# Later normalization of the next batch's rows, and other places for a few loads, in a two-layer graph kernel

## The chip, the core and the metric

The kernel runs on one core of one Trainium2 chip. The metric is device time in microseconds (us) of one execution, lower is better. The median of 3 runs of the kernel before is 2356.52 us (2349.64 to 2357.53). The profile is of one further execution with a span of 2362.4 us.

## The reference, cut to what matters

32 graphs (batches) of 512 nodes and 512 features go through two layers; all is float32.

```python
# x, adj: (32, 512, 512); W: (512, 1024); Wqk: (512, 1024); Wv: (512, 512)
h = maximum(layernorm(x), 0)                       # layer 0
agg = (adj @ h) / maximum(sum(adj, -1), 1e-6)
x = x + relu(concat([h, agg], 2) @ W.T)
h = maximum(layernorm(x), 0)                       # layer 1
q, k = split(h @ Wqk); v = h @ Wv
agg = adj @ (k * mask)
w = mask * sum(q * agg, -1) / sqrt(512)
x = x + softmax(w, axis=1)[:, :, None] * v
```

## The kernel before

For every batch i TensorE goes through four stages of products, each done by seven instead of eight block products (Strassen's scheme, so every stage also needs sums of blocks before it, on VectorE and GpSimd):

- U(i): adj times the masked h of layer 1, 56 matmuls
- Y(i+1): h of layer 0 times half of W, 56 matmuls, for the next batch
- O(i): layer 0's output, 112 matmuls, in 14 steps of 8
- TV(i-1): layer 1's two products of h (a matrix made of Wq and Wk, and Wv), 98 matmuls, in 14 steps of 7

After O(i) come TV(i-1), U(i), Y(i+1) and O(i+1). The program orders the work of all engines by hand: `p.at(n, f)` puts f into the instruction streams just after step n of the stage.

In a stage of the kind of O the products share three PSUM tiles. `copy` is an instruction of ScalarE (ACT in the profile); a product that comes back to a tile has to wait for the copy of what stands in it.

```python
def product(name, terms, place, finish):
    # m(k, p, first): 2 terms of 4 or 8 matmuls into p, one step (yield) after each
    pp = mm_tile(...)
    yield from m(1, pp, True)            # O: steps 0, 1
    c11 = place(0, 0); copy(c11, pp)
    pr = mm_tile(...)
    yield from m(2, pr, True)            # steps 2, 3
    finish(0, 0, c11, pr, c11)
    yield from m(6, pp, False)           # steps 4, 5
    c12 = place(0, 1); copy(c12, pp)
    pq = mm_tile(...)
    yield from m(5, pq, True)            # steps 6, 7
    m5 = block(...); copy(m5, pq)
    yield from m(7, pp, False)           # steps 8, 9
    c22 = place(1, 1); copy(c22, pp)     # stands in ACT's stream between steps 9 and 10
    finish(1, 1, c22, m5, c22)
    yield from m(3, pq, False)           # steps 10, 11
    finish(0, 1, c12, pq, c12)
    yield from m(4, pp, False)           # steps 12, 13: waits for the copy of c22
    finish(1, 0, None, pp, None)
```

While TensorE works on batch i, the rows of batch i+2 are made ready. x and adj come in through two half tiles ("n", two buffers for both): x is normalized in place and written to DRAM, from where it is read back transposed; then adj comes into the same two buffers.

```python
def half_tile(name):
    return big.tile([P, 2, 512], F32, tag="n", bufs=2, name=name)

class FrontH:                     # h of layer 0
    def load(self, h): self.n[h] = half_tile(...); half_rows(self.n[h], x[self.b], h)    # 4 DMAs
    def stats(self, c): ...                                     # VectorE: bn_stats, bn_aggr
    def write(self, c):
        normalize(v, v, self.t, c)                              # ACT: Relu, scale rstd, bias nmr
        nc.sync.dma_start(out=self.to.d[c], in_=v)
# variance(t): rstd, VectorE then GpSimd (pow); shift(t): nmr, VectorE
class FrontA:                     # adj
    def load(self, h): self.n[h] = half_tile(...); half_rows(self.n[h], adj[self.b], h)  # 4 DMAs
    def sum(self, c): nc.scalar.activation(v, v, AF.Copy, accum_out=DEG[...])            # ACT
    def degrees(self, h): ...                                                            # VectorE
    def write(self, c): nc.scalar.activation(v, v, AF.Copy, scale=self.rdeg[...]); nc.sync.dma_start(...)
class FrontH1:                    # h of layer 1
    def keep(self): nc.sync.dma_start(out=self.x1, in_=X[self.b]...)   # x after layer 0, 1 MB to DRAM
    def write(self, c): normalize(...); nc.sync.dma_start(...)
    def mask(self, c): nc.scalar.activation(..., scale=mraw[...])
```

In layer 1's product TV, product 1 takes four PSUM tiles (of eight), product 2 four more, and product 5 takes over those of product 2 (steps 6 and 7). ACT copies product 1, product 6 and product 5 out of PSUM; product 3 (steps 10 and 11) waits for the copies of product 5 (`m_tv` in the profile).

The main loop, cut:

```python
weights, mvR = start()          # ends with the "joint product" of Wq and Wk; it also takes h1 of batch 0
for i in range(B):              # B = 32
    if i > 0:
        p = Plan()
        for n in range(4): p.at(2 * n + 1, stream.load)      # DMA of a weight block
        ...
        p.at(9, post.store, 0); p.at(11, post.store, 1)      # output of batch i-2, 4 DMAs each
        for k in range(4): p.at(2 + k, f1.inner_sums, k, 0, 7)   # VectorE, 1 to 2 us each
        if 1 < i and i + 2 < B:                              # i = 2 to 29
            fh = FH[i + 2]
            for c in range(C):                               # C = 4
                p.at(3 + c, fh.stats, c)
                p.at(8 + c, fh.write, c)
            p.at(6, variance, fh.t)
            p.at(7, shift, fh.t)
        p.at(11, th.turn, 0)
        if 1 < i and i + 2 < B:
            fa = FA[i + 2] = FrontA(i + 2)
            p.at(12, fa.load, 0)
            p.at(13, fa.load, 1)
        p.at(12, f.stats, 0); ...
        run(layer0_out(i, stream.take), 14, p)               # O(i)

        p = Plan()
        for c in range(C):
            p.at([2, 3, 5, 6][c], f.write, c)
            p.at(8 + c, f.mask, c)
        p.at(1, f.keep)
        if 1 < i and i + 2 < B:
            for h in range(2):
                for c in range(2): p.at(4 + 2 * h + c, fa.sum, 2 * h + c)
                p.at(7 + 2 * h, fa.degrees, h)
        ...
        run(layer1_tv(i - 1), 14, p)                         # TV(i-1)
    ...
    run(layer1_u(i), 7, p)                                   # U(i)
    run(layer0_y(i + 1), 7, p)                               # Y(i+1)
```

Of the kernel before, what the change touches and what calls it, by code (L numbers as in the profile page):

```python
# [22 lines left out]
def kernel(  # L23
# [37 lines left out]
    C = N // P  # L61
# [53 lines left out]
    def of(t):  # L115
        return lambda i: t[:, i]
# [526 lines left out]
    FH, FA, F1 = {}, {}, {}  # L643
# [6 lines left out]
    def chain(p, f, n):  # L650


        p.at(n(0), f.keep)
        p.at(n(0), f.stats, 2)
        p.at(n(0), shift, f.t, 0, 2)
        p.at(n(0), f.write, 0)
        p.at(n(1), f.stats, 3)
        p.at(n(1), variance, f.t, 2, 4)
        p.at(n(1), f.write, 1)
        p.at(n(2), shift, f.t, 2, 4)  # L660
        p.at(n(3), f.write, 2)
        p.at(n(3), f.mask, 0)
        p.at(n(4), f.write, 3)
        p.at(n(4), f.mask, 1)
        p.at(n(5), f.masked_sums, 0)
        p.at(n(5), f.mask, 2)
        p.at(n(6), f.mask, 3)

    def start():
# [3 lines left out]
        fa = FA[0] = FrontA(0)  # L673
# [9 lines left out]
        fh = FH[1] = FrontH(1)  # L683
# [45 lines left out]
        p = Plan()  # L729
# [23 lines left out]
        p = Plan()  # L753
# [39 lines left out]
        f = F1[0] = FrontH1(0)  # L793
# [7 lines left out]
        p = Plan()  # L801
# [34 lines left out]
        p.at(12, f.to.read, 0)  # L836
        p.at(13, f.to.read, 1)
        FH[2] = FrontH(2)
        p.at(4, FH[2].load, 0)
        p.at(6, FH[2].load, 1)  # L840
        run(None, 14, p)
        return [right_sums(outer)[k] for k in range(4)] + [right_sums(inner)[k] for k in range(4)], mv

# [5 lines left out]
    with tc.manual_schedule(engines=engines):  # L849
        weights, mvR = start()  # L850
        post = None
        for i in range(B):
# [3 lines left out]
            f = F1[i]  # L856
            if i > 0:

                p = Plan()
                for n in range(4):  # L860
                    p.at(2 * n + 1, stream.load)
                right_y = right_sums(of(Y[i]), nc.gpsimd)
                p.at(0, right_y[0])
                p.at(0, right_y[2])
                for k in (1, 3):
                    p.at(1 + k // 2, FA[i].sums, k, nc.gpsimd)
                    p.at(1 + k // 2, right_y[k])
                if i == 1:
                    for k, g in enumerate(weights[4:]):
                        p.at(3 + 2 * k, g)  # L870
                    fa = FA[2]
                    for h in range(2):
                        for c in range(2):
                            p.at(2 * h + c, fa.sum, 2 * h + c)
                            p.at(4 + 2 * h + c, fa.write, 2 * h + c)
                        p.at(2 + 2 * h, fa.degrees, h)
                    FH[3] = FrontH(3)
                    p.at(9, FH[3].load, 0)
                    p.at(10, FH[3].load, 1)
                f1 = F1[i - 1]  # L880
                for k in range(4):
                    p.at(k // 2, f1.sums, k)
                if post is not None:
                    for c in range(C):
                        p.at(2 + c, post.apply, c)
                    p.at(3, post.add_x1, 0)
                    p.at(5, post.add_x1, 1)
                    p.at(9, post.store, 0)
                    p.at(11, post.store, 1)
                for k in range(4):  # L890
                    p.at(2 + k, f1.inner_sums, k, 0, 7)
                if 1 < i and i + 2 < B:
                    fh = FH[i + 2]
                    for c in range(C):
                        p.at(3 + c, fh.stats, c)
                        p.at(8 + c, fh.write, c)
                    p.at(6, variance, fh.t)
                    p.at(7, shift, fh.t)
                if more:
                    th = FH[i + 1]  # L900
                    p.at(2, th.to.read, 1)
                    p.at(11, th.turn, 0)
                if 1 < i and i + 2 < B:
                    fa = FA[i + 2] = FrontA(i + 2)
                    p.at(12, fa.load, 0)
                    p.at(13, fa.load, 1)
                p.at(12, f.stats, 0)
                p.at(12, f.stats, 1)
                p.at(13, variance, f.t, 0, 2)
                run(layer0_out(i, stream.take), 14, p)  # L910


                post = Post(i - 1, F1[i - 1])
                p = Plan()
                p.at(0, f.stats, 2)
                p.at(0, shift, f.t, 0, 2)
                p.at(0, f.stats, 3)
                p.at(1, variance, f.t, 2, 4)
                if last:
                    p.at(1, FA[i].factor)  # L920
                p.at(3, shift, f.t, 2, 4)
# [4 lines that stand above are left out]
                for k in range(4):  # L926
                    p.at([10, 12, 12, 12][k], f.masked_sums, k)
                if 1 < i and i + 2 < B:
                    for h in range(2):
                        for c in range(2):  # L930
                            p.at(4 + 2 * h + c, fa.sum, 2 * h + c)
                        p.at(7 + 2 * h, fa.degrees, h)
                if i == 1:
                    fa = FA[3] = FrontA(3)
                    p.at(11, fa.load, 0)
                    p.at(13, fa.load, 1)
                    fh = FH[3]
                    for c in range(C):
                        p.at(4 + c, fh.stats, c)
                        p.at(9 + c, fh.write, c)  # L940
                    p.at(7, variance, fh.t)
                    p[9].insert(0, lambda t=fh.t: shift(t))
                if more:
                    p.at(3, th.turn, 1)
                    for k in range(4):
                        p.at(5 + k // 2, th.sums, k)
                p.at(8, f.to.read, 0)
                p.at(9, f.to.read, 1)
                for k in range(7):
                    p.at(12 + k // 4, post.recombine, k, 0, 0)  # L950
                run(layer1_tv(i - 1), 14, p)


            p = Plan()
# [7 lines left out]
            if i == 0:  # L962
                fh = FH[2]
                for c in range(C):
                    p.at(c, fh.stats, c)
                p.at(3, variance, fh.t)
                p.at(4, shift, fh.t)
                p.at(4, weights[0])
                p.at(5, fh.write, 0)
                p.at(6, fh.write, 1)  # L970
                p.at(5, weights[1])
            elif more:
                for k in range(7):
                    p.at(1 + k // 4, post.recombine, k, 1, 0)
                for c in range(C):
                    p.at(3 + c // 2, post.dot, c)
                p.at(5, post.scores)
                p.at(5, post.maximum)
                if i == 1:
                    for c in range(C):  # L980
                        p.at(3 + c, fa.sum, c)
                    p.at(5, fa.degrees, 0)
                elif i + 2 < B:
                    for c in range(C):
                        p.at(c, fa.write, c)
                if 1 < i and i + 3 < B:
                    FH[i + 3] = FrontH(i + 3)
                    p.at(6, FH[i + 3].load, 0)
            else:
                p.at(0, f.turn, 0)  # L990
                for k in range(3):
                    p.at(1, f.inner_sums, k, 0, 2)
                p.at(1, f.turn, 1)
                for k in range(4):
                    p.at(2 + k // 2, f.sums, k)
                p.at(4, f.inner_sums, 3, 0, 2)
                for k in range(4):
                    p.at(5 + k // 2, f.inner_sums, k, 2, 7)
# [3 lines left out]
            if more:  # L1002
                p = Plan()
# [14 lines left out]
                        p.at(3 + k // 2, post.recombine, k, None, 1)  # L1018
                p.at(2, FA[i].factor)
                if i == 0:  # L1020
                    p.at(0, fh.write, 2)
                    p.at(1, fh.write, 3)
                    p.at(4, weights[2])
                    p.at(6, weights[3])
                    FA[2] = FrontA(2)
                    p.at(2, FA[2].load, 0)
                    p.at(3, FA[2].load, 1)
                elif i == 1:
                    p.at(0, fa.degrees, 1)
                    for c in range(C):  # L1030
                        p.at(2 + c, fa.write, c)
                    FH[4] = FrontH(4)
                    p.at(5, FH[4].load, 0)
                    p.at(6, FH[4].load, 1)
                elif i + 3 < B:
                    p.at(0, FH[i + 3].load, 1)
# [3 lines left out]
        p = Plan()  # L1040
# [71 lines left out]
```

## Time and profile before

| | busy, us | share of the span |
|---|---|---|
| TensorE, matmuls (PE) | 2269.6 | 96% |
| TensorE, weight loads (PEld) | 1977.3 | 84% |
| VectorE (DVE) | 1988.7 | 84% |
| ScalarE (ACT) | 1026.2 | 43% |
| GpSimd (POOL) | 504.8 | 21% |

The DMA engines moved 463.65 MB, at a mean of 196 GB/s. Names in the profile are those of the tiles, without numbers: `pp_o` is the tile pp of stage O, `n` a half tile with x, `a` one with adj, `nmr` the bias of a normalization, `ptv` the PSUM tiles of TV. An arrow points from what is read to what is written. A line number such as L100 is often that of a helper: L100 is `copy`, L258 `normalize`, L467 the matmuls of TV, L130 those of the other stages.

### The profile page before, as it was taken

Reading aid. Unit: us, or ns where it says so; the run is one execution under the profiler, and the core shown is the slowest. Engines: PE = TensorE matmul, PEld = TensorE weight load, DVE = VectorE, ACT = ScalarE, POOL = GpSimd, SP = SyncE. Lnnn points to the kernel's source line nnn. Section 1 sums busy time; section 2 is a strip of 40 time slices with the busy share of each in tenths; the row PEclk is TensorE's granted clock in tenths of the full one; section 3 lists DMA queues with packets and bytes.
Section 4 is the critical chain, followed back from the end, with each engine's and each line's share of the span. In section 5 each row is a group of like instructions: output and inputs, shape, how many; then the busy total and the mean of one; then the engine's idle time right before and its main releaser. Section 6 shows DMA issues by size and latency. Waiting matters only on the chain.

```text
span 2362.4 us, 32559 instructions
## 1 busy us (share of the span) xinstructions
PE 2269.6 (96%) x10372; PEld 1977.3 (84%) x10372; DVE 1988.7 (84%) x3619; ACT 1026.2 (43%) x1903; POOL 504.8 (21%) x453
## 2 busy tenths in 40 slices
PE   7998999999999999999999999999999999999996
PEld 6787888888888888888888888888888888888885
DVE  6788888888888888888788888888888888888878
ACT  4454434444334444344444344443444443444332
POOL 0212222112222122222022221222220222211222
PEclk9999999999999999999999999999999999999998
DMA  9877777887777887777877777777778777787552
GB/s 225 236 196 209 200 185 186 218 217 198 197 185 198 222 217 187 204 186 203 220 198 199 185 198 209 210 201 201 177 208 220 210 200 190 184 218 201 147 135 71
DMA packets 409594, 463.65 MB, mean 196 GB/s; under 512 B 37680, under 2 KB 271152, under 8 KB 405328
## 3 DMA queue, kind: packets, MB, share of 16 engines
q1 hardware_dynamic: 400176, 428.56, 68.0%
q0 software_dynamic: 8928, 32.51, 7.5%
q8 instruction: 82, 1.34, 0.3%
q14 instruction: 88, 0.72, 0.1%
q10 hardware_dynamic: 320, 0.52, 0.1%
HBM read 293.93 MB, written 167.51 MB: 195 GB/s over the span
## 4 chain that ended last, share of the span: by engine, by line
PE 43%; DVE 33%; DMA 11%; issue 5%; SPq 4%; ACT 2%; POOL 1%; DVEq 0%; ACTq 0%
PE ptv L467 26%; DVE h1T L97 11%; PE pp_o L130 6%; DVE tv L94 6%; PE pp_u L130 5%; DMA daT<-a 4%; DVE st L242 3%; DMA n<-in_x_dram 3%; DVE aT L280 3%; SPq L212 2%; PE pr_u L130 2%; DVE h1T L94 2%; DVE y L94 1%; SPq L204 1%; POOL rstd L248 1%
## 5 line engine op out<-in xcount | busy, mean ns | idle before, releaser
L467 PE MATMUL ptv<-mv,h1T 128*128 128x256 f32 x3136 | 682.6, 379 | 1.4 <-DVE h1T L97 1.2
L467 PEld LDWEIGHTS ptv<-mv,h1T 128*128 128x128 f32 x3136 | 595.7, 190 | 83.1 <-DVE h1T L97 1.6
L94 DVE TENSOR_TENSOR tv<-tv 128x256 f32<-128x256 f32 (+1 forms) x644 | 321.8, 511 | 11.6
L100 ACT ACTIVATE tv<-ptv 128x512 f32<-128x512 f32 (+1 forms) x372 | 189.5, 540 | 259.2 <-PE ptv L467 254.8
L130 PE MATMUL pp_o<-w,wide 128*128 128x256 f32 x992 | 246.8, 393 | 53.8 <-ACT o L100 53.8
L97 DVE TENSOR_TENSOR h1T<-h1T 128x512 f32<-128x512 f32 (+2 forms) x195 | 292.0, 1511 | 1.2
L130 PEld LDWEIGHTS pp_o<-w,wide 128*128 128x128 f32 x992 | 191.3, 195 | 91.0 <-ACT o L100 65.0
L130 PE MATMUL pp_o<-y,aT 128*128 128x256 f32 x1024 | 248.4, 386 | 1.1 <-POOL y L97 1.1
L130 PE MATMUL pp_y<-wide 128*128 128x256 f32 x1024 | 242.8, 380 | 0.0
L130 PE MATMUL pp_u<-h1m,aT 128*128 128x256 f32 x1024 | 242.0, 379 | 0.0
L130 PEld LDWEIGHTS pp_o<-y,aT 128*128 128x128 f32 x1024 | 200.2, 196 | 30.6 <-POOL y L97 1.5
L97 POOL TENSOR_TENSOR y<-y 128x512 f32<-128x512 f32 x124 | 217.8, 1757 | 19.2 <-DVE y L94 15.8
L130 PEld LDWEIGHTS pp_y<-wide 128*128 128x128 f32 x1024 | 195.0, 191 | 26.8 <-ACT y L100 0.3
L130 PEld LDWEIGHTS pp_u<-h1m,aT 128*128 128x128 f32 x1024 | 194.5, 190 | 27.1 <-issue 0.5
L248 POOL TENSOR_TENSOR rstd<-rstd,mhalf 128x2 f32<-128x2 f32 (+1 forms) x96 | 78.6, 819 | 545.1 <-DVE rstd L247 545.1
L548 POOL PARTITION_ALL_REDUCE gtop<-top x32 | 12.5, 392 | 854.0 <-DVE top L545 836.1
L100 ACT ACTIVATE y<-pp_y 128x512 f32<-128x512 f32 x128 | 76.4, 597 | 238.4 <-PE pp_y L130 238.4
L258 ACT ACTIVATE n<-n,nmr,rstd 128x512 f32<-128x512 f32 x120 | 91.0, 804 | 176.7 <-DVE nmr L252 173.8
L100 ACT ACTIVATE xu<-pp_u 128x512 f32<-128x512 f32 x128 | 76.4, 597 | 194.5 <-PE pp_u L130 194.5
L94 DVE TENSOR_TENSOR tv<-ptv,tv 128x512 f32<-128x512 f32 x248 | 142.6, 612 | 17.1 <-PE ptv L467 13.4
L100 ACT ACTIVATE o<-pp_o 128x512 f32<-128x512 f32 x96 | 56.7, 591 | 216.9 <-PE pp_o L130 216.9
L94 DVE TENSOR_TENSOR tv<-ptv,m_tv 128x512 f32<-128x512 f32 (+1 forms) x124 | 76.7, 623 | 80.8 <-PE ptv L467 68.3
(113 smaller groups left out, 3457.7 us busy)
## 6 DMA issues: line engine op xcount, KB each, us to landing
w<-dw SPq DMA_DIRECT2D x217, 256.0 KB, 3.2
xu<-in_x_dram SPq DMA_DIRECT2D x128, 256.0 KB, 5.0
a<-in_adj_dram SPq DMA_DIRECT2D x256, 128.0 KB, 3.5
dx<-xu SPq DMA_DIRECT2D x32, 1024.0 KB, 5.2
dh1T<-h1m SPq DMA_DIRECT2D x128, 256.0 KB, 4.3
sh1T<-dh1T SPq DMA_DIRECT2D x256, 128.0 KB, 3.2
shT<-dhT SPq DMA_DIRECT2D x248, 128.0 KB, 4.4
daT<-a SPq DMA_DIRECT2D x124, 256.0 KB, 3.0
```

The costliest lines, as they stand in the source:

```text
L94: (on or nc.vector).tensor_tensor(o, a, b, op=ALU.add)
L97: (on or nc.vector).tensor_tensor(o, a, b, op=ALU.subtract)
L100: nc.scalar.activation(o, i, AF.Copy)
L130: nc.tensor.matmul(p[:, rc, :], lt[:, LEFT[k], dk, ts(rc, P)], right[:, dk, :], start=first and n == 0, stop=True, skip_group_check=True,)
L204: nc.sync.dma_start(out=t[q * R:(q + 1) * R, :, :], in_=rows[:, 2 * h:2 * h + 2, :])
L212: nc.sync.dma_start(out=t[q * R:(q + 1) * R, :, :], in_=src[:, :, ts(q, P)].rearrange("k r j -> r k j"))
L242: nc.vector.bn_stats(st, src)
L248: nc.gpsimd.tensor_tensor(rstd[:, a:b], rstd[:, a:b], mhalf[:, a:b], op=ALU.pow)
L258: nc.scalar.activation(o, i, AF.Relu, scale=t[1][:, c:c + 1], bias=t[2][:, c:c + 1])
L280: nc.vector.transpose(o, self.s.pop(h).rearrange("p k (c r) -> p k c r", r=R))
L467: nc.tensor.matmul(banks[n][:, :, ts(i, P)], left[:, LEFT[k], LEFT_IN[j], :], mvR[:, RIGHT[k], RIGHT[j], :, :], start=first and i == 0, st ...
L548: nc.gpsimd.partition_all_reduce(self.gtop, self.top, channels=P, reduce_op=ReduceOp.max)
```

## The change

The change has five parts. It adds and removes no instruction; all move.

- In O(i), i from 2 to 29, the normalization and the write of the next rows of x move two steps later, from steps 8 to 11 to steps 10 to 13, and with them the small operations before them (variance from 6 to 7, shift from 7 to 9). Its aim is that the normalization stands at the end of O in place of its middle.
- For the same i the second half of adj is asked for in step 1 of TV, behind the 1 MB write of `keep`, in place of step 13 of O.
- In the joint product at the start, `keep` of batch 0 stands two places later (behind the first two writes of h1), and the loads of batch 2's x stand at 10 and 12 in place of 4 and 6.
- Batch 2's rows of x are measured two steps later in U(0), and all four are normalized and written in Y(1) in place of two in U(0) and two in Y(1); one load of adj and the sums of weights there move with them.
- In O(1) the sums, degrees and writes of batch 2's adj stand two steps later, the loads of batch 3's x one step later.

```diff
@@ chain: joint product
-        p.at(n(0), f.keep)
+        p.at(n(2), f.keep)
@@ start: joint product
-        p.at(4, FH[2].load, 0)
-        p.at(6, FH[2].load, 1)
+        p.at(10, FH[2].load, 0)
+        p.at(12, FH[2].load, 1)
@@ O(1)
-                            p.at(2 * h + c, fa.sum, 2 * h + c)
-                            p.at(4 + 2 * h + c, fa.write, 2 * h + c)
-                        p.at(2 + 2 * h, fa.degrees, h)
+                            p.at(2 + 2 * h + c, fa.sum, 2 * h + c)
+                            p.at(6 + 2 * h + c, fa.write, 2 * h + c)
+                        p.at(4 + 2 * h, fa.degrees, h)
-                    p.at(9, FH[3].load, 0)
-                    p.at(10, FH[3].load, 1)
+                    p.at(10, FH[3].load, 0)
+                    p.at(11, FH[3].load, 1)
@@ O(i), i = 2 to 29
-                        p.at(8 + c, fh.write, c)
-                    p.at(6, variance, fh.t)
-                    p.at(7, shift, fh.t)
+                        p.at(10 + c, fh.write, c)
+                    p.at(7, variance, fh.t)
+                    p.at(9, shift, fh.t)
                     p.at(12, fa.load, 0)
-                    p.at(13, fa.load, 1)
@@ TV(i-1), i = 2 to 29
+                    p.at(1, fa.load, 1)
@@ U(0)
-                    p.at(c, fh.stats, c)
-                p.at(3, variance, fh.t)
-                p.at(4, shift, fh.t)
-                p.at(4, weights[0])
-                p.at(5, fh.write, 0)
-                p.at(6, fh.write, 1)
-                p.at(5, weights[1])
+                    p.at(2 + c, fh.stats, c)
+                p.at(5, variance, fh.t)
+                p.at(6, shift, fh.t)
+                p.at(6, weights[0])
@@ Y(1)
-                    p.at(0, fh.write, 2)
-                    p.at(1, fh.write, 3)
-                    p.at(4, weights[2])
-                    p.at(6, weights[3])
+                    for c in range(C):
+                        p.at(c, fh.write, c)
+                    for k in range(1, 4):
+                        p.at(3 + k, weights[k])
-                    p.at(2, FA[2].load, 0)
-                    p.at(3, FA[2].load, 1)
+                    p.at(3, FA[2].load, 0)
+                    p.at(6, FA[2].load, 1)
```

## The prediction, made before the changed kernel ran

> **What bounds the kernel now.** I read the shares of busy time first, then TensorE's own waits, then the chain of work, then the timeline of one batch. TensorE is busy for 96% of the span, so what can be won is TensorE's idle time. Its waits are few:
>
> ```profile
> PE pp_o L130 <- ACT o L100: 53.8, 28, 5.9
> PE h L635 <- ACT h L707: 14.0, 2, 13.5
> PE pr_u L130 <- ACT h1m L379: 2.0, 1, 2.0
> ```
>
> (us in total, times, longest.) There are 28 waits of stage O for a copy by ACT, and 28 batches (i = 2 to 29) in which O carries the normalization of batch i+2. The chain of waits tells their whole cost:
>
> ```profile
> 201.86 21.15 PE ptv L467 x98
> ...
> 2146.79 21.15 PE ptv L467 x98
> 2192.12 3.45 PE pp_o L130 x16
> ...
> 2216.29 21.15 PE ptv L467 x98
> 2285.79 18.14 PE ptv L467 x84
> ```
>
> (Start, us, work.) From one TV to the next in the last batches, where O carries no normalization, it is 2285.79 - 2216.29 = 69.50 us. From 201.86 to 2146.79 there are 27 such periods, of 72.03 us each: 1944.9 - 27 x 69.5 = 68.4 us are lost, 2.5 per batch. In the TensorE timeline U, Y and TV take 12.1, 12.1 and 21.15 us in all of these, so all of it is lost in O. One batch (i = 15), TensorE and ACT:
>
> ```profile
> 1127.28 1.89 PE L130 MATMUL pq_o<-y,aT 128*128 128x256 f32 x8
> 1131.41 2.95 PE L130 MATMUL pp_o<-w,wide 128*128 128x256 f32 x8 [2.25 <-ACT o L100]
> 1134.15 2.67 PE L130 MATMUL pp_o<-y,aT 128*128 128x256 f32 x8
> ```
>
> ```profile
> 1129.36 1.52 ACT L258 ACTIVATE n<-n,nmr,rstd 128x512 f32<-128x512 f32 x2 [6.41 <-DVE nmr L252]
> 1130.79 0.57 ACT L100 ACTIVATE o<-pp_o 128x512 f32<-128x512 f32 x1
> 1131.27 1.51 ACT L258 ACTIVATE n<-n,nmr,rstd 128x512 f32<-128x512 f32 x2
> ```
>
> Product 7 ended at 1125.6, so c22 could be copied then. But its copy stands behind two normalizations, ACT sits idle for 6.41 us before them until VectorE has made nmr, and product 4 (the second `pp_o` row) waits 2.25 us for the copy at 1130.79. Its 16 matmuls then take 5.3 us where 3.45 is normal. The windows show why:
>
> ```profile
> 1130.00:1133.00 3.00, 1.58 (x6) 1.33 (x7) 1.57 (x3) 2.77 (x5) 0.00 (x0) 0.88 0.64 183
> 1133.00:1136.00 3.00, 3.00 (x9) 2.42 (x8) 2.93 (x4) 0.00 (x0) 0.00 (x0) 0.55 1.00 316
> ```
>
> (Stretch, length, busy PE, PEld, DVE, ACT, POOL, granted clock, DMA share, GB/s.) The granted clock was 0.55 after the wait. And the DMA engines are full there, which the rivals below rest on.
>
> **What the Trainium skill says.** "PSUM — Partial Sum Buffer", section "Engine vs sequencer instructions": the queues of ScalarE and VectorE are strictly first in, first out. The trace agrees: the copy, ready at 1125.6, ran 5.2 us later, behind the normalizations. "TensorE: Matmul & The Clock Gate", section "What's actually happening": the array's default state is throttled to half its clock, and activity over windows of about 3.4 us lifts it. The trace agrees in kind (0.55), though here a gap of 2.25 us was enough, and only in some batches: O loses 4.1 to 4.3 us in eight of the 27, 1.1 to 2.6 in the others. "DMA: Bandwidth & Descriptors", section "Two DMAs through the same engine are not ordered": a dependent DMA must be held back at its issue until the first one's semaphore. So a load of adj into a half tile holds the whole SP queue until the write of x from it has landed; the trace has dhT<-n at 2.9 us from issue to landing.
>
> **The change, part by part.** The order of instructions on each engine, built but not run, shows these moves.
>
> (1) In O, ACT: the copy of c22 now stands ahead of all four normalizations. It starts at 1125.6 and ends at 1126.2; product 4 needs it at 1129.0 (end of product 3). The wait of 2.25 us goes, and the slow clock with it. The order on VectorE does not change, so nmr still ends at 1129.3; the normalizations run from 1129.4 to 1132.4, and TV starts at 1129.0 + 3.45 = 1132.4 in place of 1136.7. ACT is free just in time for TV's first copy (1.1 us later). Gain: the 68.4 us of 27 batches. O(2) loses 9.7 us now (5.87 in this wait, 1.08 in one for GpSimd, the rest slow clock), of which about 8 go.
>
> (2) VectorE loses its own wait for that copy (`o<-m_o,o` waited 2.07 us from 1129.3), but TV comes 4.3 us earlier, so VectorE is about 2.2 us later against TensorE. In i = 15 it reads the last `pp_o` until 1137.8; 2.07 earlier is 1135.7, TV + 3.3, and its bank is wanted at the earliest in TV's step 3 (TV + 4.5): 1.2 us to spare. Its additions of product 2 end at TV + 8.65 and are wanted at 9.1 and 10.6. They fit.
>
> (3) SP: the new order is write 0, four stores, writes 1 and 2, four loads of adj, write 3, `keep`, four loads, writes of h1. With the means of the timeline (measured from U's start; write 1 landed at 51.0, first half of adj landed 5.1 after its first issue, second 4.95, the last write 2.6) the first half is asked for at 51.1 and lands at 56.2; write 3 lands at 55.9; the second half is asked for then and lands at 60.9 to 61.5. TV starts at 48.35. So the halves land at TV + 7.9 and TV + 12.5 to 13.1. ACT is free for the first sum at about TV + 5.5 and so waits 2.4 us (it waits 1.5 on average now: 38.5 us in 26 waits), and reaches the third sum at TV + 12.55 or up to 0.5 later. Now the third sum starts at TV + 11.4 and the last `m_tv` copy ends 3.06 later; then it ends at TV + 15.6 to 16.2. Product 3 wants the first two `m_tv` at TV + 15.1 (they end at 14.3 to 14.9) and the last two at 16.6. It fits with 0.2 to 0.8 us. DMA landings scatter by about 1 us, so some batches will miss: I put 0.25 us for each of 27, 7 us in all.
>
> (4) O(2): VectorE is some 5 us further behind there (nmr at 193.8, product 3 ended at 190.0), so TV(1) will wait about 3 us for banks that VectorE has not read. Of the 8 us, 5 stay.
>
> (5) The start: U(0) waits 2.0 us for a mask that waits for h1's last write, which stands behind `keep` and four loads now; that wait goes. But VectorE is busy without a break from 77 to 158 us and does not get earlier (it waits for the second transposed half, about 79.7 as before), so the 2 us come back as waits in O(1) and TV(0). Net 0, give or take 3.
>
> Sum: 68.4 + 5 - 7 + 0 = 66 us. 2356.5 - 66 is 2290; I take 2293, as all that is uncertain in (3) costs time.
>
> **The rivals.** A: a new wait takes the place of the one removed. The half of adj lands later than I work out, the sums hold up ACT, and product 3 waits in TV for `m_tv`. For it: the DMA engines are full around that time (shares of 1.00 at 1133 to 1136, 1.05 at 1142 to 1145), and the margin is under 1 us. Against it: a delay of all landings by 1 us costs TensorE only some 0.5 us. If it costs 1.5 us in each batch plus slow clock, 45 us come back and the time is about 2330. B: VectorE becomes the bound, as its 1988.7 us of work now have to fit into fewer us and it enters TV later. For it: 62 of 69.5 us are busy. Against it: it still sits idle twice per batch, 2.6 us before product 7's addition in TV and 3.31 us before the first addition in Y, where it catches up, so nothing is carried into the next batch. If it is wrong, 1 us per batch, 2320. C: the clean case, with no new wait at all and 8 us from O(2): 2280. D: the moves at the start lose time, at most 5 us.
>
> **Range and chances.** The clean case and a good start give 2278 as the low end; A at a little over half its size gives 2325 as the high end. Faster by over 2% means under 2309.4, a residue below about 0.9 us per batch: 0.75. Within 2%: 0.22. Slower needs a new wait of over 4 us in each batch: 0.03.
>
> **What would show it.** Right: the 28 waits of `pp_o` for ACT are gone, and O takes 24.2 us in every batch from i = 3; the period from TV to TV is 69.5 to 70. The first sum of adj on ACT waits over 2 us in TV. VectorE's wait for `o<-m_o` has gone, and its idle time before `pr_y` is smaller. Wrong: TensorE waits for `m_tv` copies (L100) or for VectorE's additions in `ptv`, in nearly every batch; or nmr itself comes later, because the transposed adj lands later, and `pp_o` waits on something else.

## The result and the profile after

| | median, us | lowest to highest | runs |
|---|---|---|---|
| before | 2356.74 | 2349.64 to 2357.53 | 4 |
| after | 2293.94 | 2292.68 to 2295.82 | 4 |

The ratio is 0.9741, with a 95% interval of 0.9721 to 0.9761. The profiled execution spans 2292.1 us. The kernel before scatters by 7.9 us in these runs and by 21.7 us over 31 runs of one comparison (2345.8 to 2367.5); why is seen below.

TensorE's own waits in the kernel after; the columns are us in total, times, longest:

```profile
PE h L635 <- ACT h L707: 13.9, 2, 13.4
PE pp_y L130 <- ACT y L100: 2.9, 1, 2.9
PE ptv L467 <- ACT m_tv L100: 2.8, 2, 2.0
...
PE pp_o L130 <- ACT o L100: 0.5, 1, 0.5
```

All 28 waits for the copy of c22 (53.8 us) are gone. The one of 0.5 us in O(1) is new, and so are two waits for `m_tv`, one for a copy in Y(1) and one of 1.1 us for a load of weights in O(2). The wait for `h` belongs to the start and is what it was.

The chain of work that ended last, TensorE's rows of TV (start, us, work):

```profile
267.52 21.15 PE ptv L467 x98
...
1101.66 21.24 PE ptv L467 x98
...
2145.94 21.15 PE ptv L467 x98
```

From 267.52 to 2145.94 there are 27 periods: 1878.42 us, 69.57 each where 69.50 is the time without any wait. They lose 1.9 us in sum, where 27 periods of the kernel before lost 68.4. The row at 1101.66 is one that lost 0.09 us. The last whole TV stage starts at 2145.94, where the kernel before starts it at 2216.29: the 70.35 us of difference are the difference of the spans, so nothing is won or lost after it.

Batch i = 15 again, TensorE and then ACT (start, us, operation; in brackets the idle time before it and what ended it):

```profile
1096.32 1.89 PE L130 MATMUL pq_o<-y,aT 128*128 128x256 f32 x8
1098.05 1.89 PE L130 MATMUL pp_o<-w,wide 128*128 128x256 f32 x8
1099.77 1.89 PE L130 MATMUL pp_o<-y,aT 128*128 128x256 f32 x8
```

```profile
1094.85 0.60 ACT L100 ACTIVATE o<-pp_o 128x512 f32<-128x512 f32 x1 [2.86 <-PE pp_o L130]
1097.02 2.93 ACT L258 ACTIVATE n<-n,nmr,rstd 128x512 f32<-128x512 f32 x4 [1.57 <-DVE nmr L252]
...
1109.80 0.63 ACT L330 ACTIVATE a<-a 128x512 f32<-128x512 f32 x1 [3.07 <-DMA a<-in_adj_dram]
...
1115.34 0.63 ACT L330 ACTIVATE a<-a 128x512 f32<-128x512 f32 x1 [1.08 <-DMA a<-in_adj_dram]
1115.87 0.18 ACT L330 ACTIVATION_READ_ACCUMULATOR a<-a 128x1 f32 x1
1115.96 1.06 ACT L100 ACTIVATE m_tv<-ptv 128x512 f32<-128x512 f32 x2
```

The copy of c22 (1094.85) waits for its product alone; then ACT waits 1.57 us for nmr, in front of all four normalizations, and holds up nobody. TensorE has no gap before 1098.05. The price is paid in TV: ACT waits 3.07 us for the first half of adj and 1.08 for the second, and the `m_tv` copies stand right behind them. Its wait for adj, all batches:

```profile
ACT a L330 <- DMA a<-in_adj_dram: 110.1, 60, 4.1
```

That was 38.5 us in 26 waits. ACT is busy for 45% of the span, and nearly all of this time costs nothing. The window of the end of O (length, PE, PEld, DVE, ACT, POOL, granted clock, DMA share, GB/s) shows no drop of the clock:

```profile
1098.00:1101.00 3.00, 3.00 (x15) 2.64 (x15) 2.93 (x5) 1.95 (x3) 0.00 (x0) 1.00 0.91 297
```

A table of what each stage loses against its matmuls at full rate (their number times 21.15/98 us), from TensorE's timeline, tells where the time went:

| | before | after |
|---|---|---|
| U(0) loses | 2.35 | 0.0 |
| Y(1) loses | 0.16 | 3.21 |
| O(1) loses | 0.0 | 0.89 |
| TV(0) starts at | 122.0 | 123.8 |
| O(2) loses | 9.71 | 1.48 |
| TV(1) starts at | 201.7 | 195.2 |
| TV(1) loses | 0.0 | 2.68 |
| O(3) to O(29) lose | 68.4 | 0.0 |
| TV(2) to TV(28) lose | 0.0 | 1.9 |

### The profile page after: what moved, and what is told of

The parts are those of the page before. It is cut to its first block, busy times and chain, and to the rows that moved or that the text cites. A ratio compares the mean times of both kernels' runs of the same rounds, so it can differ in the third digit from the quotient of the medians.

```text
span 2292.1 us, 32535 instructions
## 1 busy us (share of the span) xinstructions
PE 2248.8 (98%) x10372; PEld 1967.9 (86%) x10372; DVE 1968.1 (86%) x3619; ACT 1028.0 (45%) x1903; POOL 509.2 (22%) x453
## 4 chain that ended last, share of the span: by engine, by line
PE 89%; DVE 5%; DMA 3%; SPq 1%; issue 1%; ACT 0%; POOL 0%; DVEq 0%; ACTq 0%; POOLq 0%
PE ptv L467 26%; PE pp_o L130 18%; PE pp_y L130 9%; PE pp_u L130 9%; PE pq_o L130 9%; PE pq_y L130 5%; PE pr_o L130 5%; PE pq_u L130 4%; PE pr_y L130 2%; PE pr_u L130 2%; DVE tv L94 1%; DVE wide L94 1%; DMA dhT<-n 1%; DVE st L242 1%; DMA xu<-in_x_dram 1%
## 5 line engine op out<-in xcount | busy, mean ns | idle before, releaser
L97 DVE TENSOR_TENSOR h1T<-h1T 128x512 f32<-128x512 f32 (+2 forms) x195 | 276.3, 1430 | 1.2
L130 PE MATMUL pp_o<-y,aT 128*128 128x256 f32 x1024 | 242.0, 379 | 0.0
L130 PE MATMUL pp_o<-w,wide 128*128 128x256 f32 x992 | 234.4, 379 | 0.5 <-ACT o L100 0.5
L130 PEld LDWEIGHTS pp_y<-wide 128*128 128x128 f32 x1024 | 195.2, 191 | 30.0 <-ACT y L100 3.3
L97 POOL TENSOR_TENSOR y<-y 128x512 f32<-128x512 f32 x124 | 215.3, 1736 | 14.9 <-DVE y L94 12.3
L130 PEld LDWEIGHTS pp_o<-y,aT 128*128 128x128 f32 x1024 | 194.4, 190 | 26.7 <-POOL y L97 0.3
L330 ACT ACTIVATE a<-a 128x512 f32<-128x512 f32 x128 | 80.2, 627 | 110.1 <-DMA a<-in_adj_dram 110.1
```

The source lines that it names most:

```text
L97: (on or nc.vector).tensor_tensor(o, a, b, op=ALU.subtract)
L130: nc.tensor.matmul(p[:, rc, :], lt[:, LEFT[k], dk, ts(rc, P)], right[:, dk, :], start=first and n == 0, stop=True, skip_group_check=True,)
L330: nc.scalar.activation(v, v, AF.Copy, accum_out=DEG[self.b][:, c:c + 1])
```

## The experiments

Times are medians; the ratio is to runs of the kernel before on the same chip. "U + 43.8" means 43.8 us after the start of U in the same round of stages, and "TV + 15" likewise; product 7 ends at U + 41.6, product 3 at U + 45.1, and an undelayed TV starts at U + 48.35. The theory: the order of ACT's stream was the whole loss, and its cure is worth some 66 us as long as adj lands before ACT needs it. The rivals: the gain is due to the later load of adj or to the new start, or a wait for `m_tv` eats most of it.

### e1: only the later normalization, in the kernel before

```diff
-                        p.at(8 + c, fh.write, c)
+                        p.at(10 + c, fh.write, c)
```

> The kernel before with one edit: the four normalizations of the next x stand at steps 10 to 13 of O in place of 8 to 11; the loads of adj, the small operations and the start stay. Theory (the order of ACT's stream is all): the waits of pp_o for ACT are gone from the batches 2 to 29, O takes 24.2 us in each, the ratio to before is 0.97 to 0.975. Rival (SP): with the second half of adj still asked for at the end of O, SP is held by the landing of write 3, keep and h1's writes come late, and new waits of 1 us or more per batch appear in TV or U: ratio 0.98 to 0.99. Rival (the loads are the cause): the time stays at 2350 or more.

Measured: 2291.05 us, ratio 0.9742 (0.9714 to 0.977). O(3) to O(29) lose 0.0, TV(2) to TV(28) lose 0.0, O(2) 0.8 and TV(1) 3.0 (1.5 us in a wait for VectorE, 1.0 for `m_tv`). One line of the program holds all of the gain. With adj asked for as before, its second half lands at U + 60.4 (61.4 in the changed kernel) and ACT waits for adj 71.2 us in 37 waits: the second `m_tv` copy ends at TV + 13.9 in the mean in place of 15.05, and nothing is left of the 1.9 us.

### e2: only the later load of adj; e3: only the start

```diff
 # e2, O(i) and TV(i-1)
-                    p.at(13, fa.load, 1)
+                    p.at(1, fa.load, 1)
 # e3: the five blocks of the diff outside "O(i), i = 2 to 29" and "TV(i-1)"
```

> The kernel before with one edit: the second half of adj is asked for in step 1 of TV, behind keep. Theory: ACT's stream is as before, so the 28 waits of pp_o stay at about 54 us in all and the time stays within 0.3% of before (2350 to 2363). Rival (the load order gives the gain): at least 20 us less than before.

> Only the three parts of the change that touch the joint product, U(0), Y(1) and O(1); the batches from 2 on as before. Theory: the 2.3 us won in U(0) are lost in Y(1) (a copy of y behind a normalization that waits for nmr, about 3 us) and in O(1) (about 1 us); 1 to 3 us slower than before, which is within the scatter. Rival (the start gives a part of the gain): 5 us or more less than before.

Measured: e2 2352.33 us, ratio 1.0002 (0.9984 to 1.0019); e3 2356.0 us, ratio 1.0005 (0.9991 to 1.0019). Both keep the 28 or 29 waits of the product for the copy; TensorE's waits in e2:

```profile
PE pp_o L130 <- ACT o L100: 43.0, 28, 5.7
```

That is less than the 54 us expected, in an execution that was the fastest of twelve; the median is that of the kernel before. Neither the later load nor the three parts at the start bring anything by themselves. The start of e3 shows what the new order does there by itself: U(0) loses 0, Y(1) 4.2, O(1) 0.9, and TV(0) starts at 125.8 where the kernel before has 122.0. O(3) to O(29) lose 49.5 us in e2 and 58.8 in e3, 68.4 in the profile of the kernel before, with the same order of ACT's stream. The three profiled spans rise with it (2343.8, 2355.4, 2362.4 us). So this loss varies from run to run, and it is large enough to be the scatter of the kernel before.

### e4: the copy behind one normalization

The changed kernel with the normalization one step earlier, so that one of the four stands ahead of the copy of c22.

```diff
-                        p.at(10 + c, fh.write, c)
+                        p.at(9 + c, fh.write, c)
-                    p.at(9, shift, fh.t)
+                    p.at(8, shift, fh.t)
```

> The changed kernel with its normalizations one step earlier (steps 9 to 12, shift in step 8), so that one of four, not two as before and not none, stands ahead of the copy of c22. Theory (what holds the copy is the wait for nmr, each normalization adds 0.72 us): the copy ends at nmr + 1.35 us, product 3 ends 44.9 us after U's start; with nmr at 43.85 O loses 0.4 us, with nmr at 45.2 it loses 1.75 us and some slow clock. 12 to 50 us more than the changed kernel: 2305 to 2343. Rival (ACT's own work is the cost, half of it is left): 2325 to 2330. Rival (only the order of two operations near the end matters, one normalization is hidden): 2294 to 2297.

Measured: 2329.82 us (2325.65 to 2336.19), ratio 0.9909 (0.988 to 0.9938). That is inside what the theory gave, but the first rival's 2325 to 2330 holds it too, so the total alone does not decide. The batches do. Batch i = 14, with U at 1077.7: TensorE, ACT and VectorE.

```profile
1120.87 1.89 PE L130 MATMUL pq_o<-y,aT 128*128 128x256 f32 x8
1124.30 1.99 PE L130 MATMUL pp_o<-w,wide 128*128 128x256 f32 x8 [1.54 <-ACT o L100]
```

```profile
1122.95 0.81 ACT L258 ACTIVATE n<-n,nmr,rstd 128x512 f32<-128x512 f32 x1 [6.40 <-DMA out_dram<-tv]
1123.67 0.58 ACT L100 ACTIVATE o<-pp_o 128x512 f32<-128x512 f32 x1
1124.15 2.21 ACT L258 ACTIVATE n<-n,nmr,rstd 128x512 f32<-128x512 f32 x3
```

```profile
1122.76 0.16 DVE L252 SCALAR_TENSOR_TENSOR nmr<-mv,rstd 128x4 f32<-128x4 f32 x1 [1.18 <-POOL rstd L248]
```

nmr ends at 1122.92, ACT starts its normalization 0.03 us later (the bracket names a DMA that landed about then; the one that counts is nmr), and the copy comes behind it. The copy then ends at nmr + 0.03 + 0.72 + 0.58. With nmr at U + 45.2 that is U + 46.5, 1.5 us after product 3's end; with nmr at U + 43.85 it is U + 45.2. O loses about 1.8 us in the batches of the first kind and 0.4 to 0.7 in those of the second (17 and 9 of 27; one more loses 2.2). Half of ACT's work, the rival, would have left about half of 2.5 us in each batch; instead the loss goes with nmr. O(2) loses 9.0 us, nearly all that it lost before. So one normalization costs what the idle time of ACT ahead of it costs, not its own 0.7 us.

### e5: both halves of adj late

The changed kernel with the first half of adj, too, asked for in TV, behind `keep`.

```diff
-                    p.at(12, fa.load, 0)
+                    p.at(1, fa.load, 0)     # TV(i-1)
```

> The changed kernel with the first half of adj too asked for in step 1 of TV, behind keep (SP then goes from write 3 to keep, to eight loads). Theory (the margin of adj in TV is under 1 us): the first half lands 2 us or more later than now (TV + 9.5 or later), the second about as now; the first sums and the copies behind them come 1.5 to 2 us later, product 3 waits for m_tv in most batches, 0.5 to 2 us each: 15 to 55 us more than the changed kernel. Rival (ACT has time enough in TV): within 3 us of the changed kernel.

Measured: 2325.44 us, ratio 0.9874 (0.9852 to 0.9895). TV loses 29.6 us in 27 batches, O nothing. TensorE's waits, and ACT's for adj:

```profile
PE ptv L467 <- ACT m_tv L100: 14.8, 25, 0.7
```

```profile
ACT a L330 <- DMA a<-in_adj_dram: 153.5, 31, 6.3
```

The first half is asked for at U + 51.5, as before (51.6), but behind the 1 MB write, and lands at TV + 10.3 in place of 7.4. The first `m_tv` copy then ends at TV + 16.0 in the mean, and product 3 waits for it in 25 batches. This is rival A of the prediction. A batch with TV's start at 1118.04, TensorE and ACT:

```profile
1118.04 15.89 PE L467 MATMUL ptv<-mv,h1T 128*128 128x256 f32 x70
1134.59 6.31 PE L467 MATMUL ptv<-mv,h1T 128*128 128x256 f32 x28 [0.66 <-ACT m_tv L100]
```

```profile
1133.94 1.09 ACT L100 ACTIVATE m_tv<-ptv 128x512 f32<-128x512 f32 x2
```

The row of ACT holds two copies and ends at 1135.03; product 3 starts at 1134.59, 0.05 us after the first of them has ended. So it waits for the first copy alone, which ends 0.49 us before the second. The end of that copy in each batch tells the loss of the batch (us, counted from TV's start; three kernels):

| first `m_tv` ends at | kernel | TV loses |
|---|---|---|
| 14.57, 14.71, 14.81 | after | 0.0, 0.0, 0.0 |
| 14.98, 15.04, 15.26 | after | 0.03, 0.09, 0.31 |
| 15.21, 15.51, 15.61 | after, second time | 0.27, 0.56, 0.66 |
| 16.05 | after | 1.10 |
| 15.82, 16.24, 16.74 | e5 | 0.87, 1.28, 1.79 |

In all 27 batches of each of these kernels the loss is what the first copy ends later than TV + 14.95, to within 0.01 us. This edge is where product 3 stands after its 70 matmuls at full rate, TV + 15.11, less the 0.05 us above and the 0.10 us by which the first matmul after a wait is longer. With the first copy's end at TV + 14.57 in the mean the changed kernel stands 0.4 us ahead of it. (TensorE's waits for `m_tv` add up to only 14.8 of the 29.6 us, for two reasons. 8.6 us are lost before product 3, in 16 batches, where product 7 waits for the copies of product 6 behind the first two sums. And a wait is counted from the modelled end of the last matmul, so that one of the length shown costs 0.27 us more.)

### e6: the sums of adj one step later

The changed kernel with ACT's sums where their wait ends by itself.

```diff
-                            p.at(4 + 2 * h + c, fa.sum, 2 * h + c)
-                        p.at(7 + 2 * h, fa.degrees, h)
+                            p.at([5, 6, 8, 9][2 * h + c], fa.sum, 2 * h + c)
+                        p.at(8 + 2 * h, fa.degrees, h)
```

> The changed kernel with the four sums of adj in TV at steps 5, 6, 8 and 9 in place of 4, 5, 6 and 7 (degrees one step later), so that the third stands behind the copies of product 5. Theory: the two waits for m_tv (2.8 us, one of them in TV(1)) and the lost 2 us in the batches from 3 on are gone, 3 to 5 us less than the changed kernel. Rival (the late sums hold up masks and VectorE in U): as much or more.

Measured: 2288.72 us (2287.86 to 2289.46), ratio 0.9719 (0.9695 to 0.9744), below the changed kernel's own range, though on another chip. ACT's wait for adj:

```profile
ACT a L330 <- DMA a<-in_adj_dram: 8.0, 3, 4.1
```

110.1 us of waits shrink to 8.0. With the last two sums behind the `m_tv` copies the last of these ends at TV + 13.7 in every batch, 2.7 us earlier in the mean, and TV(2) to TV(28) lose nothing; TV(1) loses 0.6 in place of 2.7 and starts at 192.8. So the residue in TV and most of TV(1)'s loss were the copies standing behind sums that wait for a load.

### e7: the two steady parts without the new start; e8: with late sums

```diff
 # e7: the kernel before with the blocks "O(i), i = 2 to 29" and "TV(i-1)" of the diff only
 # e8: e7, the sums of e6, and
-        p.at(n(0), f.keep)
+        p.at(n(2), f.keep)
```

> The two parts of the change that touch the batches from 2 on, with the start as before. Theory: O from batch 3 as in the changed kernel; TV(0) starts 1 to 2 us earlier than in the changed kernel; 0 to 3 us less than the changed kernel. Rival (the moves at the start are needed): 2 us or more slower than it.

> The kernel of the two steady parts with keep of batch 0 behind the first writes of h1 (which takes the wait out of U(0)) and the later sums. Theory: 2.3 us won in U(0) without the wait in Y(1), though VectorE may take it back in O(1); no waits for m_tv; 4 to 9 us less than the changed kernel. Rival: VectorE is busy without a break there, the time of TV(1) does not move, 3 us less than the changed kernel at most.

Measured: e7 2291.59 us, ratio 0.9733 (0.9712 to 0.9753); e8 2288.84 us, ratio 0.972 (0.9699 to 0.974). The three parts at the start bring nothing in the sum: e7 starts TV(0) at 122.9, the changed kernel at 123.8, and loses 1.3 us in TV. In e8 U(0) still loses 2.8 us: the move of `keep` alone does not take the wait for the mask away.

### The start: the changed kernel again, e9 and e10

What the new start wins in U(0) is lost in Y(1). The changed kernel's Y(1), TensorE and ACT:

```profile
85.20 1.89 PE L130 MATMUL pr_y<-wide 128*128 128x256 f32 x8
90.04 1.99 PE L130 MATMUL pp_y<-wide 128*128 128x256 f32 x8 [2.94 <-ACT y L100]
```

```profile
88.69 0.81 ACT L258 ACTIVATE n<-n,nmr,rstd 128x512 f32<-128x512 f32 x1 [4.42 <-DVE nmr L252]
89.41 0.57 ACT L100 ACTIVATE y<-pp_y 128x512 f32<-128x512 f32 x1
```

This is the pattern of the kernel before's O once more: a copy that a product waits for, behind a normalization that waits 4.42 us for VectorE. e9 moves the four normalizations in Y(1) one step later; e10 also takes the sums of e6, and in O(1) puts the last two of the four writes of adj (which wait for rdeg) behind the copy of c22; the first two stay ahead of the copy `m_o`.

```diff
 # e9, Y(1)
-                        p.at(c, fh.write, c)
+                        p.at(1 + c, fh.write, c)
 # e10: e9, the sums of e6, and in O(1)
-                            p.at(6 + 2 * h + c, fa.write, 2 * h + c)
+                            p.at([6, 7, 10, 11][2 * h + c], fa.write, 2 * h + c)
-                    p.at(10, FH[3].load, 0)
-                    p.at(11, FH[3].load, 1)
+                    p.at(9, FH[3].load, 0)
+                    p.at(12, FH[3].load, 1)
```

> The changed kernel again, on the chip of the next three, for comparison: 2291 to 2296.

> The changed kernel with the four normalizations of batch 2 in Y(1) one step later (1 to 4), so that the first copy of y stands ahead of them. Theory on Y(1): its 3.2 us are the wait of that copy for nmr; Y(1) loses 0.5 us at most. Theory on what follows (VectorE is busy without a break until about 158 us and sets the pace): the 3 us come back in O(1), at the copy of c22 behind adj's writes, or in TV(0) and O(2), and TV(1) starts within 1 us of where it starts in the changed kernel (195.2). Rival (TensorE's order sets the pace): TV(1) starts about 3 us earlier.

> The changed kernel with later sums in TV, the later normalizations in Y(1), and in O(1) the last two writes of adj behind the copy of c22 (steps 10 and 11; loads of batch 3's x at 9 and 12). Theory (VectorE sets the pace at the start): Y(1) and O(1) lose nothing, TV(0) starts 3 us earlier than in the changed kernel, but waits for VectorE appear in TV(0) or O(2); TV(1) starts at 191 to 193, 2286 to 2289 in all. Rival: the whole of Y(1) and O(1) is won, TV(1) starts at 189, 2284 or less.

Measured, all on one chip: the changed kernel 2296.04 us (2292.56 to 2298.95), ratio 0.9757 (0.9736 to 0.9778); e9 2295.05 us, ratio 0.9754 (0.9739 to 0.977); e10 2288.93 us, ratio 0.9728 (0.9714 to 0.9743). In e9 Y(1) loses 0.24 in place of 4.40, but O(1) loses 2.6 in place of 0.9. O(1) of e9, TensorE and ACT:

```profile
115.61 1.99 PE L130 MATMUL pq_o<-w,wide 128*128 128x256 f32 x8 [1.63 <-ACT m_o L100]
...
119.81 1.99 PE L130 MATMUL pp_o<-w,wide 128*128 128x256 f32 x8 [0.48 <-ACT o L100]
```

```profile
113.74 1.33 ACT L343 ACTIVATE a<-a,rdeg 128x512 f32<-128x512 f32 x2 [6.03 <-DVE rdeg L335]
114.98 0.57 ACT L100 ACTIVATE m_o<-pq_o 128x512 f32<-128x512 f32 x1
```

A third case of the same pattern, now with rdeg: TensorE comes earlier, VectorE does not, and the wait moves to the next copy behind an operation that waits for VectorE. TV(1) starts at 195.5; that is level with the changed kernel's first profile (195.2), but 2.3 us earlier than its profile on this chip (197.8), so e9 leaves open whether a little was won. In e10 Y(1) loses 0, O(1) 1.3 where nothing was expected (1.05 us in the wait for `m_o`), TV(0) 0.5, O(2) 0.3, and TV(1) starts at 192.8 and loses 1.2 (a wait for VectorE's additions). That is 7.1 us below the changed kernel on the same chip. But e6, which moves the sums alone and still loses 2.8 us in Y(1), starts TV(1) at 192.8 as well. So what the moves in Y(1) and O(1) are worth by themselves is not shown, and that VectorE sets the pace at the start is not ruled out.

### e11: only two edits in the kernel before

The edit of e1 together with the sums of e6.

> The kernel before with two edits only: normalizations at steps 10 to 13 of O, and the later sums of adj in TV. Theory: everything that the change brings comes from the first edit, and the second takes away the wait of TV(1) (3.0 us with the first edit alone, 1.5 of it for VectorE, 1.0 for m_tv): 2287 to 2291, below the changed kernel. Rival (the other parts of the change are needed): above it.

Measured: 2292.15 us (2290.12 to 2292.45), ratio 0.974 (0.9725 to 0.9754), 1 us above what was expected. TV loses 0.6, as it should, but O(2) loses 4.2, of which 2.3 in a wait for GpSimd's additions; e1 loses 0.8 there, and why this differs stays open. Over a whole run the start decides between 2288.7 and 2292.

All versions, with the stages that tell them apart:

| | median, us | TV(1) starts | TV(1) loses | O(3..29) | TV(2..28) |
|---|---|---|---|---|---|
| after | 2293.94 | 195.2 | 2.7 | 0.0 | 1.9 |
| e1 | 2291.05 | 193.4 | 3.0 | 0.0 | 0.0 |
| e6 | 2288.72 | 192.8 | 0.6 | 0.0 | 0.0 |
| e7 | 2291.59 | 194.7 | 1.7 | 0.0 | 1.3 |
| e8 | 2288.84 | 194.7 | 1.6 | 0.0 | 0.0 |
| e10 | 2288.93 | 192.8 | 1.2 | 0.0 | 0.0 |
| e11 | 2292.15 | 196.6 | 0.4 | 0.0 | 0.6 |

e6, e8 and e10 beat both kernels, each by 5 us or more over the changed one (only e10 was timed on one chip with it); they can't be told apart from each other.

## Why the prediction was right

The time was predicted as 2293 (2278 to 2325) and is 2293.94. That it came within 1 us is in part luck: the 68.4 us were read from a profile whose span is some 8 us over that of a median run, and taken off the median; the 5 us too many in step (3) and the 3 us added for caution made up for that. Step by step:

**Step (1), the copy of c22, was right.** It was to start when product 7 ends, and starts at U + 41.70 in all 27 batches; O takes 24.17 us in each. The 68.4 us of the profile are gone. About 48 of them were the waits themselves (53.8 less O(2)'s 5.87). Some 13 were matmuls at a lower clock, in eight of the batches. The other 7, 0.27 in each batch, are what the count of a wait leaves out: O loses 2.51 us where the wait is 2.24 and the clock stays up. e1 shows that moving the normalizations alone brings the gain, e2 and e3 that none of the other parts does. In medians the gain is 62.8 us, less than the 70.3 between the two profiles, because the profiled execution of before (2362.4) was one of its longer ones.

**Step (2), VectorE fits, was right.** Its last read of `pp_o` ends at U + 50.2 in the median (51.6 was worked out), and TensorE waits for VectorE in TV for 1.6 us in the whole run. One thing was not foreseen: nmr comes earlier, at U + 43.85 in the median where it was 45.20, and was taken as unchanged. It is off TensorE's path now, so no time is won by it.

**Step (3), adj lands just in time, was right in its mechanism and 5 us too large in its size.** The halves land at U + 55.8 and 61.4 (56.2 and 60.9 to 61.5 predicted), the first sum is at TV + 7.6 (7.9), the third at 13.4 (12.55 to 13.05), the second `m_tv` ends at TV + 15.05 (14.3 to 14.9; wanted at 15.1), the last at 16.4 (15.6 to 16.2; wanted at 16.6). So the copies come later than worked out, and they scatter as supposed (the second one ends between 14.0 and 16.5). The term that was mis-sized is the 0.25 us for each batch, and what made it too large is which copy is wanted first: the prediction held the second `m_tv` to TV + 15.1, but e5 shows product 3 starting on the first one, which ends 0.49 us earlier, at TV + 14.57 in the mean against an edge of 14.95. (The kernel's TV has steps of 8 and 6 matmuls by turns, not of 7, so the last two copies are wanted at TV + 16.8, not 16.6.) Eight of 27 batches miss the edge, by 0.03 to 1.1 us, 0.07 in the mean of all: 1.9 us in place of 7. e6 shows that the residue is this wait, for it goes away when the sums stand behind the copies.

**Step (4), the first batches, had the right net and a wrong cause.** O(2) gains 8.2 us (8 predicted) and TV(1) loses 2.7 (3), net 5.5 (5). But TV(1) was to wait for banks that VectorE had not read. The changed kernel's TV(1), TensorE and ACT:

```profile
200.69 10.20 PE L467 MATMUL ptv<-mv,h1T 128*128 128x256 f32 x46 [0.17 <-DVE xu L442]
212.86 6.31 PE L467 MATMUL ptv<-mv,h1T 128*128 128x256 f32 x28 [1.98 <-ACT m_tv L100]
```

```profile
211.60 0.63 ACT L330 ACTIVATE a<-a 128x512 f32<-128x512 f32 x1 [2.57 <-DMA a<-in_adj_dram]
...
212.23 1.06 ACT L100 ACTIVATE m_tv<-ptv 128x512 f32<-128x512 f32 x2
```

VectorE accounts for 0.17 us of it. The 1.98 us are step (3) at its worst: ACT waits 2.57 us for the second half of adj, and the `m_tv` copies behind it come too late. The step that failed is the one that took VectorE's delay for the last wait there; e6, which moves nothing on VectorE but the small `degrees` and cures ACT's order, brings 2.7 down to 0.6.

**Step (5), the start, was right in its sum only.** U(0)'s wait goes, as predicted, and comes back, but not "in O(1) and TV(0)" through VectorE's pace alone: 2.94 us of it sit in Y(1), in a copy behind a normalization. TV(0) starts 1.8 us later (0, give or take 3). VectorE's pace may well stand behind it, since e9 moves the wait on to O(1); both waits fall on TensorE where a copy of ACT stands behind what waits for VectorE. How much moving these copies would win without the later sums of e6 stays open.

In the profiled spans the sum is 68.4 + 5.5 - 1.9 - 1.8 = 70.2 us, against the predicted 68.4 + 5 - 7 + 0 = 66. Of the rivals, A is seen at its full size in e5 only, B nowhere, and of D the 1.8 us by which TV(0) starts later. Of the signs for "wrong", none is in the profile.

## What to carry to other kernels

On an engine with a queue in order, the copy that sets an accumulating PSUM tile free belongs ahead of everything that waits for another engine or a load: such an operation can cost TensorE its idle time, not only its busy time (e4). In a profile this looks like a short copy right behind an operation with a long idle time in brackets, and a matmul whose bracket names the copy; mending one of them shows the next, so go through all stages for the pattern before counting the gain. A late load cost nothing here as long as no copy that TensorE needs stood behind its consumer; with the consumer moved behind the copy (e6), the margin of the load no longer mattered.

## What was not expected of the hardware

**VectorE's additions slow down beside GpSimd's.** With that goes the time at which nmr ends, U + 43.85 in some batches and U + 45.2 in others. The kernel before, VectorE and GpSimd at i = 15:

```profile
1119.08 2.15 DVE L97 TENSOR_TENSOR h1T<-h1T 128x896 f32<-128x896 f32 x1
...
1123.29 1.08 DVE L97 TENSOR_TENSOR h1T<-h1T 128x896 f32<-128x896 f32 x1
```

```profile
1118.17 2.11 POOL L97 TENSOR_TENSOR y<-y 128x512 f32<-128x512 f32 x1
1120.24 1.95 POOL L573 DMA_DIRECT2D tv<-dx  x2
```

The same addition of two tiles takes 2.15 us where it meets a GpSimd addition, which runs until 1120.28, and 1.08 us after GpSimd has stopped adding. The 128x512 ones take 684 ns in the mean in one place (`wide<-wide`) and 1598 ns where they run beside GpSimd (`h1T<-h1T`). The Trainium skill, "SBUF — State Buffer", section "SBUF: two separate sides", says that a VectorE operation with two SBUF inputs and a GpSimd operation that reads SBUF shut each other out for a whole instruction; the doubled times agree in kind. Eight such additions stand ahead of nmr. In the kernel before and the changed one nmr ends at U + 43.8 to 44.0 in all batches where four of them take over 1.3 us, at 44.1 to 44.5 where five do, at 45.2 to 45.3 where six do. What decides how many meet is not shown: the median of nmr is U + 43.85 in the changed kernel and 45.20 in e8, with O free of waits in both.

**The clock falls by windows of 3.41 us, not by the length of the gap alone.** In the kernel before O loses 4.1 to 4.3 us in eight of 27 batches and 2.5 to 2.6 in eight others, after gaps of the same 2.2 to 2.3 us. The windows of i = 15 (columns as above):

```profile
1128.89:1132.30 3.41, 1.16 (x6) 0.81 (x5) 1.03 (x3) 2.94 (x5) 0.24 (x1) 1.00 0.36 115
1132.31:1135.71 3.40, 3.40 (x10) 2.69 (x9) 3.33 (x5) 0.46 (x1) 0.00 (x0) 0.50 0.98 302
1135.73:1139.10 3.37, 3.37 (x17) 2.96 (x17) 3.20 (x10) 1.06 (x2) 0.70 (x1) 1.00 0.97 268
```

In each trace all changes of the granted clock lie whole multiples of 3.413 us apart, to within 5 ns, so they mark a fixed row of windows. In i = 15 the gap of 2.25 us, 1129.16 to 1131.41, lies in one window, and the clock is 0.50 in the next; in i = 16 the gap of 2.23 us is cut by the border at 1203.99 into 1.1 and 1.1 us, and the clock stays. Over the 14 profiles there are 145 gaps of TensorE over 0.8 us between 70 and 2280 us: the 23 with at least 2.04 us inside one window were all followed by a window at 0.50, the 122 with at most 1.92 us were not. So between gaps of one length it is their place in the windows that decides, and the gaps of 1.5 to 1.9 us in e4 were too short at any place.
